# Loads of x on GpSimd's queue with eight half strips in place of five, in a convolutional attention and edge-filter kernel

## The chip, the cores and the metric

The kernel runs on one core of one Trainium2 chip. The metric is the time of one execution on the device in microseconds (us), as the median of several runs. The core has five engines that run at the same time, each with its own ordered stream of instructions: TensorE (PE, with its weight loads as PEld), VectorE (DVE), ScalarE (ACT), GpSimd (POOL) and SyncE (SP). SP computes nothing: it issues DMA transfers. POOL computes a little and issues transfers too. An engine carries out its stream strictly in order, so an instruction that waits holds up everything behind it on the same engine.

## What is computed

The input is x, four images of 512 channels by 64 x 64 pixels in float32. Two layers follow each other. Layer 0 is a linear attention over 8-channel heads, once on the projections q, k, v and once on their 5 x 5 depthwise convolution followed by a pointwise one, then a projection, a normalization and a residual. Layer 1 takes edge filters of layer 0's output, four branches, a channel attention, a fusing projection with a layer norm and again a residual.

```python
q, k, v = h @ wq.T, h @ wk.T, h @ wv.T                      # h: x with channels last
dw = conv(qkv, dw_kernel)                                   # 5x5, depthwise
pw = conv(dw, pw_kernel)                                    # 1x1, in groups of 8
f = concatenate([qkv, pw]).reshape(B, -1, 24, N)
query, key_, value = relu(f[:, :, :8]), relu(f[:, :, 8:16]), f[:, :, 16:]
scores = einsum('bhdn,bhen->bhde', value_pad, key_)         # value_pad: value and a row of ones
out = einsum('bhde,bhen->bhdn', scores, query)
out = out[:, :, :-1] / (out[:, :, -1:] + EPS)
y = batchnorm(conv(out, proj_kernel)) + x                   # layer 0
...
E = stack([sobel, lap, diag, grad])                         # edge filters of y
feat = gelu(batchnorm(einsum('kbchw,koc->kbohw', E, w_branch) + b_branch))
ef = feat * sigmoid(w_att2 @ gelu(w_att1 @ mean(feat)))
z = einsum('bchw,oc->bohw', ef, w_fuse) + b_fuse
return gelu(layernorm(z)) + y                               # layer 1
```

## The kernel before

**Groups and strips.** The 512 channels of q, k and v are cut into NG = 4 groups of 128, and an image's 4096 pixels into NJ = 8 strips of 512 (j = 0 to 7). The class `Group` (L231) does one group of one image: 16 groups in all, one after the other. A group first runs `keys_and_values`: for each strip in the order `KV_ORDER` (1, 0, 2, 3, ..., 7) a key projection (`project`, L274) and a value projection (`values`, L305). Then it runs `queries`: a query projection for each strip in the order `Q_ORDER` (6, 7, 5, 4, 3, 2, 1, 0). Pieces of other work stand between the projections: transposes, scores (L342), the convolution of the rolled image (`convolve`, L418), correlations (`correlate`, L473), `fold` (L371).

**x in SBUF.** A strip of x is 128 partitions by 4 x 512 floats. It is loaded as two half strips of 128 x 1024 floats, 512 KB each, by `load_x` (L260 to L266). All 16 half strips of image 0 stay in SBUF during its four groups (most of them in the pool `x_first`). For images 1 to 3 the half strips pass through the pool `xst` (L102), which has a fixed number of slots: a load waits until the last matmul that read the slot's former half strip is done. Strips 6 and 7 are kept from the values of a group to its queries, strips 1 and 0 from its queries to the keys of the next group; the others are loaded twice in a group. That makes 300 half strips for images 1 to 3, and 316 in all.

**Queues.** SP issues most loads and stores: x, weights, `near` (the values with their neighbours, L318 and L458), heads, and the data of the later stages. POOL issues four kinds: `flat<-strip` (L288, the projected strip to DRAM), `rolled<-flat` (L295, the strip back in the layout that the convolution wants), `y<-yt` (L686) and `ef<-ef_o` (L767). POOL also builds `mat` (L253) and adds in the last stage (L876, L897). In `project`, PE's projection goes to PSUM, ACT copies it (L281 for queries and L283) and POOL stores the copy (L288).

**Who sets the order.** PE's order is the order of the text (`manual_schedule` for PE alone). The streams of the other engines, SP and POOL among them, are put in order by the framework's scheduler when the program is built. It goes by the data that each instruction needs and by when it expects engines and slots to be free. It also gives each instruction its semaphore waits. The transfers of a queue take eight semaphores in turn, so a ninth waits for the first to have landed.

**Later stages beside the groups.** While the groups of image b run, `advance` gives out pieces of three later stages of image b - 1 by an expected pace: `project_out` (L677 on PE), `edge_branches` (L754 on PE, most of DVE's and ACT's work) and `fuse_out` (L866 and L882). The last image's stages run at the end, alone.

Of the kernel before, what the change touches and what calls it, by code (L numbers as in the profile page):

```python
# [89 lines left out]
def conv_seq_kernel(  # L90
    ctx: ExitStack, tc, x, wqkv, dpk, wtab, proj, projc, pwk, bn0, consts, vec, watt1, batt1, watt2, wbr, wfuse, out
):
    nc = tc.nc
# [5 lines left out]

    front = ctx.enter_context(ExitStack())  # L100
    keep = front.enter_context(tc.tile_pool(name="keep", bufs=1))
    xst = front.enter_context(tc.tile_pool(name="xst", bufs=5))  # L102
    mini = front.enter_context(tc.tile_pool(name="mini", bufs=2))
    gw = front.enter_context(tc.tile_pool(name="gw", bufs=2))
    vals = front.enter_context(tc.tile_pool(name="vals", bufs=VALS))
# [125 lines left out]
    class Group:  # L231
# [28 lines left out]
        def load_x(self, j):  # L260
            xs[self.b, j] = []
            for n in range(2):
                pool = x_first if self.b == 0 and j not in Q_ORDER[:2] else xst
                xt = pool.tile([P, 2, 512], F32, name="xt", tag="xt")
                nc.sync.dma_start(out=xt, in_=x[self.b, j, :, 2 * n : 2 * n + 2, :])
                xs[self.b, j] += [xt[:, 0, :], xt[:, 1, :]]  # L266

        def project(self, t, j):
# [873 lines left out]
```

## Time and profile before

| | us |
|---|---|
| median of 3 runs (4826.22 to 4835.85) | 4831.98 |
| the profiled execution | 4830.43 |
| its span, first to last instruction | 4828.6 |
| image 0's groups, 0 to 650: PE busy | 620.48 |
| beside image 0's later stages, 650 to 1705: PE busy of 1055 | 1007.72 |
| 1705 to 2890: PE busy of 1185 | 1121.17 |
| 2890 to 4110: PE busy of 1220 | 1138.13 |
| the last image's stages alone, 4110 to 4829: PE busy of 719 | 636.83 |

The granted TensorE clock is 0.968 over the span. The mean busy share of the DMA engines in these five stretches is 0.68, 0.77, 0.76, 0.75 and 0.54. Of the two queues in use, SP's moved 722.43 MB and POOL's 270.07 MB.

A line of a timeline gives start and length in us, the engine, the line of the program, the operation, the tile written and the tiles read, and how many instructions are merged in it. The bracket behind it is the idle time of the engine before it and what ended that idle time. A line of the waits gives who waited for whom, the total in us, how often, and the longest. A line of the DMA issues gives the tiles, the queue, the number of issues, the size of one and, for POOL's queue, the median time from issue to landing; for SP's queue the profile doesn't give that.

### The profile page before, as it was taken

The numbers are of one execution on the slowest core, as the hardware profiler recorded it, in microseconds if no ns is written. First come the engines' busy times: TensorE is split into PE (matmuls) and PEld (weight loads), VectorE is DVE, ScalarE is ACT, GpSimd is POOL, SyncE is SP. The second block draws the span as 40 slices with busy tenths as digits, with TensorE's granted clock in tenths as the row PEclk, the third lists the DMA queues.
The fourth block names the chain that finished last, engine by engine and source line by source line (L and its number), as shares of the span: only waits on it lengthen the run. The fifth ranks groups of instructions, "written<-read, shape, count | busy, mean of one in ns | idle before, by whom it ended". The sixth has DMA issues, their size and how long they took to land. (4 is left out here: it accounts for less than half of the span.)

```text
span 4828.6 us, 86405 instructions
## 1 busy us (share of the span) xinstructions
PE 4524.3 (94%) x35900; PEld 2461.5 (51%) x35900; DVE 2107.7 (44%) x2788; ACT 1588.7 (33%) x2719; POOL 987.7 (20%) x1291
## 2 busy tenths in 40 slices
PE   8999999998999999989899999988999999799987
PEld 5554554444566554444465655444446565344433
DVE  1222222114666634311356663441116666447966
ACT  2122121002554523300245452430014545214765
POOL 2111111111121224311111121431111211111443
PEclk9999999999999999999999999999999999899998
DMA  8666679667787877777678778758668887665445
GB/s 228 186 182 183 184 239 259 176 168 192 231 240 230 260 227 220 227 198 188 175 226 255 227 250 231 226 176 223 177 184 233 243 227 227 184 168 151 155 138 172
DMA packets 498327, 998.02 MB, mean 207 GB/s; under 512 B 189160, under 2 KB 221960, under 8 KB 479504
## 3 DMA queue, kind: packets, MB, share of 16 engines
q1 hardware_dynamic: 415760, 722.43, 50.6%
q0 software_dynamic: 82176, 270.07, 20.3%
q8 instruction: 283, 4.64, 0.4%
q14 instruction: 108, 0.88, 0.1%
HBM read 710.67 MB, written 281.61 MB: 206 GB/s over the span
## 5 line engine op out<-in xcount | busy, mean ns | idle before, releaser
L274 PE MATMUL proj<-xt,w_sb 128*128 128x512 f32 x2048 | 953.0, 608 | 50.3 <-DMA xt<-in_x 28.1
L677 PE MATMUL yps<-hd,fold_sb 128*128 128x512 f32 x2048 | 910.5, 600 | 35.8 <-DMA hd<-heads 27.8
L677 PEld LDWEIGHTS yps<-hd,fold_sb 128*128 128x128 f32 x2048 | 386.4, 192 | 531.7 <-issue 466.0
L274 PEld LDWEIGHTS proj<-xt,w_sb 128*128 128x128 f32 x2048 | 380.7, 194 | 541.7 <-issue 453.9
L418 PE MATMUL cv<-rolled,mat 64*32 64x504 f32 (+2 forms) x10240 | 576.4, 598 | 33.1 <-DMA rolled<-flat 19.1
L866 PE MATMUL zps<-ef,wf_sb 128*128 128x512 f32 (+1 forms) x1056 | 469.1, 597 | 45.6 <-DMA ef<-ef 16.7
L305 PEld LDWEIGHTS val<-w_sb,xt 128*128 128x128 f32 x4096 | 472.6, 193 | 43.4 <-issue 29.9
L305 PE MATMUL val<-w_sb,xt 128*128 128x128 f32 x4096 | 487.9, 278 | 2.4 <-DVE vt L312 1.9
L754 PE MATMUL br<-maps,wbr_sb 128*128 128x256 f32 (+1 forms) x1792 | 463.6, 412 | 0.0
L682 DVE SCALAR_TENSOR_TENSOR yt<-yps,shift,xr 128x512 f32<-128x512 f32 x128 | 95.7, 749 | 804.7 <-PE yps L677 757.8
L754 PEld LDWEIGHTS br<-maps,wbr_sb 128*128 128x128 f32 x1792 | 334.8, 189 | 137.4 <-issue 96.4
L288 POOL DMA_DIRECT2D flat<-strip x256 | 144.9, 566 | 1211.9 <-ACT strip L283 1184.8
L418 PEld LDWEIGHTS cv<-rolled,mat 64*32 64x32 f32 x10240 | 196.7, 109 | 381.9 <-issue 355.3
L295 POOL DMA_DIRECT2D rolled<-flat x512 | 273.3, 538 | 558.2 <-PE cv L418 519.5
L283 ACT COPY strip<-proj 128x512 f32<-128x512 f32 x256 | 149.0, 582 | 671.3 <-PE proj L274 671.3
L473 PE MATMUL corr<-near,ckt 128*32 128x160 f32 x8192 | 336.3, 318 | 26.4 <-DMA near<-near 26.2
L866 PEld LDWEIGHTS zps<-ef,wf_sb 128*128 128x128 f32 x1056 | 203.5, 196 | 293.8 <-issue 221.6
L473 PEld LDWEIGHTS corr<-near,ckt 128*32 128x32 f32 x8192 | 261.1, 112 | 122.0 <-issue 68.2
L686 POOL DMA_DIRECT2D y<-yt x128 | 114.4, 894 | 917.1 <-DVE yt L682 756.2
L730 DVE TENSOR_TENSOR maps<-dv 128x1054 f32<-128x1054 f32 (+1 forms) x112 | 159.8, 1427 | 256.8 <-PE br L754 256.7
L897 POOL TENSOR_TENSOR z<-z,yr 128x512 f32<-128x512 f32 (+1 forms) x132 | 175.5, 1348 | 272.7 <-ACT z L894 150.1
L333 ACT ACTIVATE kt<-tr 128x512 f32<-128x512 f32 x128 | 76.2, 595 | 466.4 <-PE tr L331 466.4
(131 smaller groups left out, 4466.0 us busy)
## 6 DMA issues: line engine op xcount, KB each, us to landing
xt<-in_x SPq DMA_DIRECT2D x316, 512.0 KB
near<-near SPq DMA_DIRECT2D x512, 264.0 KB
rolled<-flat POOLq DMA_DIRECT2D x512, 256.0 KB, 7.4
flat<-strip POOLq DMA_DIRECT2D x256, 256.0 KB, 5.8
win<-y SPq DMA_DIRECT2D x96, 396.0 KB
near<-vt SPq DMA_DIRECT2D x512, 66.0 KB
y<-yt POOLq DMA_DIRECT2D x128, 264.0 KB, 6.3
heads<-q SPq DMA_DIRECT2D x128, 256.0 KB
```

The lines of the kernel that those rows point to most:

```text
L274: nc.tensor.matmul(ps, lhsT=self.w[t][:, c, :], rhs=xs[self.b, j][c], start=(c == 0), stop=(c == NCH - 1))
L283: nc.scalar.copy(s, ps)
L288: nc.gpsimd.dma_start(out=self.flat[t][r, :, b : b + 8, :], in_=rows(s))
L295: nc.gpsimd.dma_start(out=self.rolled[t, half][r::8, :, :], in_=self.flat[t][r % 4, :, at : at + 8, :].rearrange("(n c) b w -> c n (b w)", ...
L305: nc.tensor.matmul(ps[:, ts(c, P)], lhsT=xs[self.b, j][n][:, ts(c, P)], rhs=self.w[VALUE][:, n, :], start=(n == 0), stop=(n == NCH - 1),)
L418: nc.tensor.matmul(rows(banks[2 * s + i])[32 * j : 32 * j + 32, :, c0:c1], lhsT=self.mat[t][q, 4 * s + j, (dx + 2) * 4 : (dx + 2) * 4 + 4, :],
L473: nc.tensor.matmul(self.banks[jj][32 * i : 32 * i + 32, 160 * b : 160 * b + 160], lhsT=self.held["c", i][:, at : at + 32], rhs=v[:, 4 * n ...
L677: nc.tensor.matmul(ps, lhsT=fold_sb[g // NG][:, g % NG, ts(c, P)], rhs=hd[g], start=(g == 0), stop=(g == 2 * NG - 1),)
L730: nc.vector.tensor_sub(flat[:, half : 3 * half - 2], dvs[:, 2 : 2 * half], dvs[:, 0 : 2 * half - 2])
L754: nc.tensor.matmul(rows(ps), lhsT=wbr_sb[:, k, c, :], rhs=rows(maps[:, slot[k], c % 2, :], WB)[:, :, 0:W], start=(c == 0), stop=(c == NCH ...
L866: nc.tensor.matmul(ps, lhsT=wf_sb[:, k, ts(c, P)], rhs=ef[k], start=(k == 0), stop=(k == 3))
L897: nc.gpsimd.tensor_add(rows(z), rows(z), rows(yr, WB)[:, :, 1 : W + 1])
```

## The change

The issue of an x load moves from SP to POOL for every image but the first, and the pool `xst` gets eight slots in place of five. Nothing else of the text changes.

```diff
@@ -99,7 +99,7 @@
     front = ctx.enter_context(ExitStack())
     keep = front.enter_context(tc.tile_pool(name="keep", bufs=1))
-    xst = front.enter_context(tc.tile_pool(name="xst", bufs=5))
+    xst = front.enter_context(tc.tile_pool(name="xst", bufs=8))
     mini = front.enter_context(tc.tile_pool(name="mini", bufs=2))
@@ -262,7 +262,7 @@
             for n in range(2):
                 pool = x_first if self.b == 0 and j not in Q_ORDER[:2] else xst
                 xt = pool.tile([P, 2, 512], F32, name="xt", tag="xt")
-                nc.sync.dma_start(out=xt, in_=x[self.b, j, :, 2 * n : 2 * n + 2, :])
+                (nc.gpsimd if self.b else nc.sync).dma_start(out=xt, in_=x[self.b, j, :, 2 * n : 2 * n + 2, :])
                 xs[self.b, j] += [xt[:, 0, :], xt[:, 1, :]]
```

PE's stream is the same before and after. In POOL's stream the 300 loads now stand among its stores and computations, where the scheduler put them. Around the end of the query strips of a group in the middle of image 1, POOL's stream then reads:

```
L288 DMACopy flat20_104<-strip_11116 128x512
L288 DMACopy flat20_104<-strip_11150 128x512
L265 DMACopy xt_11217<-in_x 128x1024
L265 DMACopy xt_11219<-in_x 128x1024
L265 DMACopy xt_11499<-in_x 128x1024
...
L265 DMACopy xt_11937<-in_x 128x1024
L288 DMACopy flat20_104<-strip_11228 128x512
```

Here `strip_11150` is the copy of the query projection of strip j = 2, and `xt_11217` and `xt_11219` are the two halves of strip j = 1.

## The prediction

> **What bounds the kernel now.** I read first the page's busy times, which say that TensorE (PE) is the bound:
>
> ```profile
> PE 4524.3 (94%) x35900; PEld 2461.5 (51%) x35900; DVE 2107.7 (44%) x2788; ACT 1588.7 (33%) x2719; POOL 987.7 (20%) x1291
> ```
>
> The span is 4828.6 us, so all that a better supply of data can return is 4828.6 - 4524.3 = 304 us. The chain that ended last covers only the final microseconds, so I went to the waits of PE, then to those of SP's queue (us in total, times, longest):
>
> ```profile
> PE proj L274 <- DMA xt<-in_x: 28.1, 4, 21.1
> PE yps L677 <- DMA hd<-heads: 27.8, 9, 10.5
> PE corr L473 <- DMA near<-near: 26.2, 11, 4.8
> ...
> SPq L265 <- PE proj L274: 270.9, 91, 16.3
> SPq L265 <- PE val L305: 225.3, 45, 25.6
> ```
>
> PE waits for x only 28.1 us in all, and 5.3 of it is the very first load, which the change leaves alone. In 650 to 4100 us, where images 1 to 3 run, it is 22.8 us in 3 waits, nearly all of it one. SP's queue does stand 270.9 + 225.3 = 496 us at L265 for a free slot, but that is time of a queue, not of PE.
>
> The big wait, in PE's timeline, and the load that ended it, in SP's (start, length):
>
> ```profile
> 3280.57 3.70 PE L274 MATMUL proj<-xt,w_sb 128*128 128x512 f32 x4 [21.12 <-DMA xt<-in_x]
> ...
> 3274.86 0.47 SPq L265 DMA_DIRECT2D xt<-in_x  x1
> ```
>
> This 512 KB load took 3280.57 - 3274.86 = 5.7 us from issue to use, on SP's queue.
>
> Then I set the changed program's order of instructions beside the timelines, at the place where a query strip of one group ends and the next begins (PE, ACT, POOL, SP around 1456 us):
>
> ```profile
> 1449.29 3.70 PE L274 MATMUL proj<-xt,w_sb 128*128 128x512 f32 x8
> 1452.92 2.54 PE L473 MATMUL corr<-near,ckt 128*32 128x160 f32 x64
> 1455.40 1.12 PE L371 MATMUL fold<-p,stt 128*128 128x512 f32 x2
> 1456.36 3.60 PE L274 MATMUL proj<-xt,w_sb 128*128 128x512 f32 x8
> ...
> 1455.76 1.17 ACT L750 ACTIVATE maps<-maps,sobel_eps 128x1048 f32<-128x1048 f32 x1
> 1456.83 0.58 ACT L281 ACTIVATE rq<-proj 128x512 f32<-128x512 f32 x1
> 1457.31 0.57 ACT L283 COPY strip<-proj 128x512 f32<-128x512 f32 x1
> ...
> 1458.18 0.55 POOL L288 DMA_DIRECT2D flat<-strip  x1 [9.46 <-ACT strip L283]
> ...
> 1437.73 0.33 SPq L265 DMA_DIRECT2D xt<-in_x  x1
> 1445.03 0.33 SPq L265 DMA_DIRECT2D xt<-in_x  x1
> ```
>
> The projection at 1449.29 is of strip j=2, the one at 1456.36 of j=1, seventh of the eight queries. Its two half strips were issued by SP at 1437.73 and 1445.03, well ahead. In the changed order both stand on POOL directly behind the store `flat<-strip` of j=2, which waits for ACT's copy, which waits for PE's projection of j=2. So they start no earlier than 1458.73, after PE wants them, though their slots were free at some 1428.
>
> **The change part by part.** *Eight slots for five* adds no instruction; it lets loads run up to four strips ahead. *The issues:* 300 half strips (316 less the 16 of image 0) leave SP, 300 x 0.35 us (median at L265) = 104 us, and with them the 496 us of slot waits; other loads of SP can only come earlier by that. PE's waits for SP's other loads in 650 to 4100 us are near 24.1, hd 17.3, ef 16.7 and watt 5.1 = 63 us; I count none as saved, as before the longest of them SP stood at L898 for POOL's z or at L318, not at L265. POOL gains 300 x 0.566 (the `flat` issue, also 128 rows) = 170 us: 988 to 1158, 24% of the span, on an engine that mostly waits. That costs nothing while POOL's next work has room; the built order also shows two more activation-table loads on ACT (1.28 us each), off the path too.
>
> *The wait removed:* the 21.1 us at 3280. In the new order that load stands far ahead (slot free at 3116, no late neighbour before it), so it goes. What is late next is `near`, whose last part was issued at 3260.4: used at 3284.2 before, it would be wanted at 3263.1 and land some 4 us after its issue, so about 3 us return. With the two small waits (1.7): gain 18 + 1 = 19 us.
>
> *The wait added.* For every xt of the new order I took the time of the POOL instruction ahead of it from the timeline, the time its slot came free (last matmul that read the slot's former tile), and the start of the matmul that wants it. Most have 20 us and more. Twelve strips don't, ten of them query j=1 of a group (all groups of images 1 to 3 but two). Start on POOL, then when PE wants it: 844.3/849.3 and 3129.8/3134.6 (second halves), 1242.2/1243.2, 1458.7/1456.4, 1672.3/1671.2, 1992.0/1994.9, 2413.5/2414.8, 2634.1/2635.2, 2851.8/2852.9, 2924.5/2929.2 (key j=3), 3822.2/3820.7, 4041.3/4041.3.
>
> The price hangs on the landing time of 512 KB on POOL's queue, which no row shows in these stages. The neighbours:
>
> ```profile
> rolled<-flat POOLq DMA_DIRECT2D x512, 256.0 KB, 7.4
> flat<-strip POOLq DMA_DIRECT2D x256, 256.0 KB, 5.8
> ...
> y<-yt POOLq DMA_DIRECT2D x128, 264.0 KB, 6.3
> ...
> ef<-ef_o POOLq DMA_DIRECT2D x16, 512.0 KB, 3.2
> ```
>
> Low end 3.2 us: the right size, but from the last stage, where DMA share is 0.54 against 0.75 to 0.77 here. High end 9.6: 7.4 plus 2.2 for another 512 KB at 222 GB/s. I take 7.0, since half the size took 5.8 to 7.4 on this queue in these stages and the full size 5.7 on SP's. Stall = start + 7.0 - wanted: 2.0, 2.2, 6.0, 9.3, 8.1, 4.1, 5.7, 5.9, 5.9, 2.3, 8.5, 7.0: sum 67 us. At 5.7 it is 51, at 9.6 it is 98, at 3.2 it is 26 (nine sites).
>
> The Trainium skill, "DMA: Bandwidth & Descriptors", section "Specifications", gives a first-byte latency of about 1 us for DMAs issued by GpSimd and 0.6 us by Sync, and its "Rules for kernel authors" say that spreading DMAs over queues saves only issue time, as all share 16 engines. The trace agrees on the issue time (POOL's is longer, 0.57 against 0.35 us) and can't show the latency by itself. By the page the load would land at 5.7 + 0.4 = 6.1 us, an estimate, and the sum would be about 56 us.
>
> *What the stalls hide.* Soon after five of these sites PE already waited for `near`, whose load is issued before the stall and gains by it: 4.8 (1256), 1.5 (1470), 3.1 (2864), 4.5 (3833), 2.2 (4056) = 16 us. These go. If the loads that now stand seven and eight in a row behind the late one slow `near`, this cover is gone, and 16 us come back.
>
> Sum: +67 - 16 - 19 = +32 us. The span is 4828.6, its execution 4830.4, the median 4832.0: 1.6 apart, so I set the sum on the median: 4864 us.
>
> **The rivals.** *A, the loads land in time (faster).* One mechanism: the late loads at the twelve sites land quickly, so that only the gain is left. It decides at a landing time of about 4 us, where stalls 34 - cover 14 - gain 19 = 0. For it: 3.2 us for 512 KB in the last stage. Against it: every median of POOL's queue in the crowded stages is above 5. With no stall: 4832 - 19 = 4813; if all 63 us of waits for SP's other loads fell too, 4750.
> *B, no difference.* Landing at 4 to 5 us, or some of SP's 63 us saved: 4832, within 10.
> *C, POOL's queue jams.* Bursts of eight loads (4 MB, 18.9 us at 222 GB/s) stand ahead of `flat` and `rolled`, and convolutions wait. For it: seven loads in a row behind each late one. Against it: from the last `rolled` issue to the convolution I read 12 to 20 us against 7.4 to land, and the bursts come when the next `rolled` is 20 us off. One convolution in each of 12 groups late by half a burst: 12 x 9.4 = 113, 4864 + 113 = 4977.
> *That the change does nothing* is excluded: the loads stand on POOL, eight deep.
>
> **How the numbers follow.** Forecast 0.72, A 0.13, B 0.10, C 0.05. The forecast's own range: landing 5.7 with the cover, 51 - 16 - 19 = +16 (4848), to landing 9.6 without it, 98 - 19 = +79 (4911). To hold 8 in 10 I reach down to 4828 (landing 3.2: 26 - 12 - 19 = -5, and B) and stop at 4900, leaving out A and the top. A measurement tells 0.2%, about 10 us, from no change: faster 0.13, same 0.10, slower 0.77.
>
> **What would show it.** PE proj waiting for xt: 22.8 us before in 650 to 4100, some 70 after, in about twelve waits of 2 to 9 us at the query before the last of each group, none of 21. PE corr's wait for near: 24 down to about 8. xt on POOL's queue: landing near 7 us. SP's waits at L265 gone. I am wrong if xt lands under 4 us, if the waits at j=1 are not there, or if PE's new time stands at convolutions (C) or SP's other loads.

## The result, and the profile after

The changed kernel takes 4963.24 us (median of 4 runs, 4953.84 to 4965.59) where the kernel before took 4832.64 beside it: 130.6 us more, a ratio of 1.0268 with a 95% interval of 1.0251 to 1.0286. The direction was forecast, the size was not: +32 had been the sum, and 4900 the top of the range. The profiled execution took 4960.89 us, its span is 4959.1 and the granted clock 0.960.

Busy times of the changed kernel:

```profile
PE 4545.5 (92%) x35900; PEld 2462.5 (50%) x35900; DVE 2104.5 (42%) x2788; ACT 1591.7 (32%) x2721; POOL 1143.5 (23%) x1591
```

PE is 21 us busier with the same matmuls, and 4959.1 - 4545.5 = 413.6 us idle in place of 304: some 109 us are new waits and 21 are slower matmuls. POOL is busy 156 us longer, near the forecast of 170; what that costs by itself no run shows. What PE waits for in the changed kernel:

```profile
PE proj L274 <- DMA xt<-in_x: 97.1, 19, 13.0
PE over L396 <- DVE rec L381: 36.4, 15, 11.6
PE corr L473 <- DMA near<-near: 25.5, 3, 11.5
PE cv L418 <- DMA rolled<-flat: 24.5, 5, 7.3
...
PE cv L418 <- DMA ef<-ef_o: 7.8, 1, 7.8
PE cv L418 <- DMA xt<-in_x: 6.7, 1, 6.7
```

The 21.1 us wait is gone, and x is now the largest wait all the same. `near` keeps its total, but as one wait of 11.5 us among three and not as many small ones. The reciprocals (17.2 before) are new in the list. The last two lines are waits for `rolled` as well: these two convolutions, at 757 and 2848 us, started directly after their last load of `rolled` had landed, 18.5 and some 23 us after its issue, where the median is 6.5 us. The profile puts the wait down to another transfer of POOL's queue that uses one of the same semaphores. So the convolutions waited 39.0 us for `rolled`, against 19.1 before. The landings on POOL's queue:

```profile
xt<-in_x POOLq DMA_DIRECT2D x300, 512.0 KB, 9.0
rolled<-flat POOLq DMA_DIRECT2D x512, 256.0 KB, 6.5
flat<-strip POOLq DMA_DIRECT2D x256, 256.0 KB, 4.5
```

One late strip, at the place that the prediction showed at 1456 us (timelines of PE, ACT and POOL of the changed kernel):

```profile
1480.95 3.70 PE L274 MATMUL proj<-xt,w_sb 128*128 128x512 f32 x8
...
1500.90 3.46 PE L274 MATMUL proj<-xt,w_sb 128*128 128x512 f32 x4 [12.72 <-DMA xt<-in_x]
1505.10 1.98 PE L274 MATMUL proj<-xt,w_sb 128*128 128x512 f32 x4 [0.73 <-DMA xt<-in_x]
...
1488.97 0.57 ACT L283 COPY strip<-proj 128x512 f32<-128x512 f32 x1
...
1489.84 0.55 POOL L288 DMA_DIRECT2D flat<-strip  x1 [9.46 <-ACT strip L283]
1490.38 3.67 POOL L265 DMA_DIRECT2D xt<-in_x  x7
```

The chain is the one that was forecast: POOL waits 9.46 us for ACT's copy, stores the strip, and only then issues seven loads in a row, the first of which PE wants at once. PE starts 1500.9 - 1490.4 = 10.5 us after that issue. Two things stand here that the prediction did not count. The second half strip is waited for again (0.73 us), and the first four matmuls take 3.46 us, where eight take 3.70 at 1480.95. The same stretch by windows, with the granted clock in the last column but two:

```profile
core 0: us, PE busy (x) PEld busy (x) DVE busy (x) ACT busy (x) POOL busy (x), PEclk, DMA share, GB/s
1470.00:1488.00 18.00, 16.50 (x118) 8.57 (x115) 15.04 (x19) 8.51 (x15) 5.05 (x9) 1.00 0.75 212
...
1500.80:1504.00 3.20, 3.10 (x4) 1.17 (x4) 0.00 (x0) 0.00 (x0) 0.00 (x0) 0.51 1.03 267
1504.00:1507.00 3.00, 2.27 (x5) 0.68 (x4) 0.00 (x0) 0.00 (x0) 0.00 (x0) 1.00 0.89 350
```

After the wait PE runs at a clock of 0.51 for some 3 us and then at 1.00 again: a long wait is paid a second time, at the restart.

**Where the time went.** PE's stream is the same in both kernels, so each matmul of one trace can be set against the same matmul of the other; the last one starts 131.5 us later. Sorted by the matmul in front of which the gap grew, with the places of the kernel before:

| part | forecast, us | measured, us |
|---|---|---|
| waits for late x strips (12 places forecast, 11 found) | +67 | +87.6 |
| extra time of the 8 matmuls after each of these waits | 0 | +28.3 |
| waits for `near` that these stalls hide | -16 | -16.0 |
| the wait at 3280, less what `near` takes back | -19 | -21.1 + 11.5 = -9.6 |
| everything else (rest of the sum) | 0 | +41.2 |

In "everything else" the largest are two waits for the reciprocal (+7.5 at 1367 and +11.6 at 3944), `watt_sb` (+8.3 at 2980), `rolled` and `ef` in front of a convolution (+6.9 at 2763), `maps` at 2547 (+5.8), and -10.5 for a load of heads at 2080. Of the 41.2 us, 9.4 had come about by 650 us, in image 0's groups, where only eight of the 300 moved loads are issued, four of them after 614 us. In e2 below, which has no load on POOL and loses nothing in all, it was 9.8. So this part can't be put down to loads on POOL.

### The profile page after: what moved, and what is told of

The parts are those of the page before. It is cut to its first block, busy times and chain, and to the rows that moved or that the text cites. A ratio compares the mean times of both kernels' runs of the same rounds, so it can differ in the third digit from the quotient of the medians.

```text
span 4959.1 us, 86522 instructions
## 1 busy us (share of the span) xinstructions
PE 4545.5 (92%) x35900; PEld 2462.5 (50%) x35900; DVE 2104.5 (42%) x2788; ACT 1591.7 (32%) x2721; POOL 1143.5 (23%) x1591
## 3 DMA queue, kind: packets, MB, share of 16 engines
q1 hardware_dynamic: 372560, 565.12, 38.7%
## 5 line engine op out<-in xcount | busy, mean ns | idle before, releaser
L274 PE MATMUL proj<-xt,w_sb 128*128 128x512 f32 x2048 | 970.4, 617 | 119.3 <-DMA xt<-in_x 97.1
L274 PEld LDWEIGHTS proj<-xt,w_sb 128*128 128x128 f32 x2048 | 384.9, 196 | 623.7 <-issue 529.4
L473 PE MATMUL corr<-near,ckt 128*32 128x160 f32 x8192 | 331.7, 315 | 29.0 <-DMA near<-near 25.5
L281 ACT ACTIVATE rq<-proj 128x512 f32<-128x512 f32 x128 | 76.1, 595 | 510.8 <-PE proj L274 448.5
```

The lines of the kernel that those rows point to most:

```text
L274: nc.tensor.matmul(ps, lhsT=self.w[t][:, c, :], rhs=xs[self.b, j][c], start=(c == 0), stop=(c == NCH - 1))
L473: nc.tensor.matmul(self.banks[jj][32 * i : 32 * i + 32, 160 * b : 160 * b + 160], lhsT=self.held["c", i][:, at : at + 32], rhs=v[:, 4 * n ...
```

## The experiments

Every run is compared with runs of the kernel before on the same chip; the ratio is what counts, since the kernel before itself took 4803 to 4832 us there. Four columns sum up the profiles: PE's wait for x at its projections (L274 in the kernel before), for `near` and for the reciprocal, and SP's wait for the store `near<-vt` at the loads of `near` (L458). Lines of runs with added text have higher numbers.

| run | x loads of images 1 to 3 | ratio (95%) | x | near | rec | SP near<-vt |
|---|---|---|---|---|---|---|
| before | SP, 5 slots | 1 | 28.1 | 26.2 | 17.2 | 68.8 |
| after | POOL, 8 slots | 1.0268 (1.0251 to 1.0286) | 97.1 | 25.5 | 36.4 | 132.4 |
| e1 | POOL, 5 slots | 1.0444 (1.0416 to 1.0473) | 195.4 | 34.1 | 14.3 | 100.4 |
| e2 | SP, 8 slots | 0.9990 (0.9974 to 1.0005) | 5.3 | 29.3 | 17.2 | 67.7 |
| e3 | POOL, j=1 on SP | 1.0156 (1.0121 to 1.0191) | 44.1 | 26.5 | 45.0 | 139.9 |
| e4 | POOL, asked for one strip earlier | 1.0127 (1.0097 to 1.0156) | 24.4 | 53.1 | 35.3 | 138.1 |
| e5 | POOL, two strips earlier | 1.0087 (1.0057 to 1.0118) | 12.8 | 49.1 | 35.6 | 129.8 |
| e6 | ACT | 1.0125 (1.0088 to 1.0162) | 5.4 | 32.8 | 23.5 | 93.2 |
| e7 | keys POOL, queries SP | 1.0066 (1.0043 to 1.0089) | 10.2 | 20.8 | 40.3 | 124.0 |
| e8 | POOL, the store flat on ACT | 1.0166 (1.0127 to 1.0206) | 31.1 | 57.4 | 22.7 | 116.7 |
| e9 | as e5, a quarter of the bytes | 0.9916 (0.9891 to 0.9941) | 5.5 | 21.7 | 17.2 | 69.4 |
| e10 | as e2, a quarter of the bytes | 0.9885 (0.9856 to 0.9914) | 5.0 | 15.1 | 17.2 | 45.3 |
| e11 | as e5, win on ACT | 1.0089 (1.0066 to 1.0112) | 14.8 | 41.2 | 25.8 | 143.7 |
| e12 | queries POOL, keys SP | 1.0044 (1.0021 to 1.0067) | 8.3 | 38.7 | 19.1 | 79.5 |
| e13 | as after, a quarter of the bytes | 1.0040 (1.0020 to 1.0060) | 56.9 | 14.8 | 17.2 | 58.8 |

A wait that the table leaves out is that of the convolutions for transfers of POOL's queue: 19.1 us before, 39.0 after, 25.1 in e2, 43.0 in e5, 28.3 in e6, 42.1 in e7, 21.7 in e12, 24.4 in e9 and 21.0 in e10.

### The two parts of the change, each alone (e1, e2)

```diff
 # e1, against the changed kernel
-    xst = front.enter_context(tc.tile_pool(name="xst", bufs=8))
+    xst = front.enter_context(tc.tile_pool(name="xst", bufs=5))
 # e2, against the changed kernel
-                (nc.gpsimd if self.b else nc.sync).dma_start(out=xt, ...
+                nc.sync.dma_start(out=xt, ...
```

> The issue engine alone is changed (loads of images 1 to 3 on POOL), the five slots stay. Theory (the loss is loads of x that stand on POOL behind a store or a copy that waits for the strip just computed, and so start too late; every stall costs start + landing - wanted): with five slots far fewer loads can be placed early. Set against the times of the kernel before, the built order has some 54 half strips with less than 9 us from their start to their use, 353 us in all at a landing of 9 us (197 at 5.7), counting both halves of a strip, so perhaps two thirds of it in PE's waits. Expected 5000 to 5180 us, and PE proj waiting for xt 180 to 350 us. Rival 1 (POOL's queue is at fault by its load alone, 300 loads of 512 KB in a FIFO with flat and rolled, wherever they stand): as the changed kernel, 4940 to 4980. Rival 2 (the eight slots are at fault, bursts of prefetches that take DMA from near and rolled): as the kernel before, 4820 to 4850.

> The eight slots alone, loads on SP as before. Theory (loss is in the issue order on POOL): no half strip of the built order has under 12 us from start to use, so the 21 us wait for xt at 3280 goes, near behind it gives some 11 back, and nothing is added: 4810 to 4830, faster than before by 0 to 0.5%. Rival 1 (POOL's queue by its load): the same, 4810 to 4830. Rival 2 (slots, bursts of prefetches): most of the 130 us stay, 4900 to 4965.

e1 took 5047.73 us and waits 195.4 us for x in 22 waits, both within its forecast. That the issue on POOL costs 4.4% with five slots and 2.7% with eight excludes rival 2: the slots do not hurt, they give the loads room. e2 confirms it from the other side. With eight slots on SP the 21.1 us wait is gone and nothing of the 130 us is there; the gain of 0.1% is no more than the measurement can tell from none.

### Earlier loads on the same queue (e3, e4, e5, e8)

```diff
 # e3: the late strips alone on SP
+                (nc.gpsimd if self.b and j != 1 else nc.sync).dma_start(out=xt, ...
 # e4: in project(), ahead of the matmuls
+            if t == QUERY and self.b and j != Q_ORDER[-1]:
+                ahead = Q_ORDER[Q_ORDER.index(j) + 1]
+                if (self.b, ahead) not in xs:
+                    self.load_x(ahead)
 # e5: as e4, with
+                ahead = Q_ORDER[min(Q_ORDER.index(j) + 2, len(Q_ORDER) - 1)]
 # e8: the store of the strip leaves POOL
-            nc.gpsimd.dma_start(out=self.flat[t][r, :, b : b + 8, :], in_=rows(s))
+            nc.scalar.dma_start(out=self.flat[t][r, :, b : b + 8, :], in_=rows(s))
```

> As the changed kernel, but the strips j=1 (the seventh query of a group, where ten of the twelve late strips were) are loaded from SP; 263 of 300 loads stay on POOL. Theory: by the built order the late sites of j=1 are gone; what is left with under 9 us is some 11 half strips near 1700-1730, 2433 and 2890-2915, 54 us at a landing of 9 us, of which some 35 reach PE. With the early loss in image 0 of 10 us and near's 11 against the 21 gained: 4850 to 4890. Rival 1 (POOL's queue by its load, 263/300 of the loss): 4940 to 4965. Rival 2 (slots): 4940 to 4970.

> As the changed kernel, with all 300 loads on POOL in eight slots, but the kernel's text asks for the next query strip's load one projection earlier, so that it stands ahead of the store of the strip just computed and not behind it. Theory: the leads at j=1 rise from some -2 to 3 us to some 4 to 11; at a landing of 9 us 44 us are short over both halves (14 at 7 us), of which some 30 reach PE: 4850 to 4890, and PE proj waiting for xt some 30 us in place of 97. Rival 1 (POOL's queue by its load): no change, 4940 to 4980. Rival 2 (slots): no change, 4940 to 4980.

> As the changed kernel (300 loads on POOL, eight slots), but the text asks for the strip after the next query strip, so that by the built order only 5 half strips have under 9 us from start to use (13 us in all), in place of 23 (164 us). Theory 1 (late strips are the whole loss): PE proj waits for xt under 15 us and the time is 4820 to 4845. Theory 2 (late strips are about half of it; the other half is that loads free of SP's order go out in bursts and take the DMA engines from SP's store near<-vt, so the reads near<-near that wait for it come late, pile up and hold up win and the reciprocals behind it): xt under 15 us as well, but SP's L458 waiting for near<-vt stays at 130 to 140 us (68.8 before), PE's waits for near stay at 45 to 60 and for rec at some 35, and the time stays at 4870 to 4895.

> As the changed kernel, but the store flat<-strip goes out on ACT's queue, directly behind the copy that makes the strip; the loads of x stay on POOL. It takes away the instruction that eight of the eleven late strips stood behind; three (behind ef<-ef_o at 2635 and 2853, y<-yt at 849) stay. Theory: half strips with under 9 us fall from 23 (164 us) to 15 (61 us); PE proj waiting for xt 97 down to 30 to 50, the time 4885 to 4920. Rival (the landing of 9 us and up in POOL's queue, and not what stands ahead of the load, makes them late): xt stays at 80 to 100 and the time at 4940 to 4970.

All 300 loads stay on POOL in e4, e5 and e8, and the time falls by 1.4, 1.8 and 1.0% of the kernel before. So the queue's load by itself (rival 1) is not the cause of that part: what counts is behind which instruction the load stands. e8 is the most direct: only the store is taken from in front of the loads, and the wait for x goes from 97.1 to 31.1 us, as forecast. e4, at 4893.22 us, lies just above its 4850 to 4890. e3 was slower than forecast (4905.02 against 4850 to 4890); 270 of its loads were on POOL, not 263. Two places that the built order showed as late stayed (in the times of the kernel before): 13.2 us at 2913, a key strip behind `ef<-ef_o`, and 6.8 us at 1731.

e5 separates two causes. The waits for x are at 12.8 us, 5.3 of them the first load of all, and still 0.87% remains: 4859.89 us, some 10 under theory 2's 4870 to 4895 and above theory 1's 4820 to 4845. The kernel before took 4810.35 us there; 1.0087 of 4832 would be 4874, inside theory 2's range. The waits are those that theory 2 named, and one that it did not name, of convolutions behind POOL's queue:

```profile
PE corr L477 <- DMA near<-near: 49.1, 10, 15.0
PE over L400 <- DVE rec L385: 35.6, 15, 10.9
...
PE cv L422 <- DMA xt<-in_x: 17.1, 2, 9.5
...
PE proj L278 <- DMA xt<-in_x: 12.8, 5, 5.3
```

The line of the convolutions stands for `rolled` again: its last loads in front of the two waits landed 19.5 and 24.4 us after their issue. With the other waits for `rolled` (25.9) that is 43.0 us, 17.9 more than in e2, where `near` and the reciprocal have 19.8 and 18.4 less than here (waits for heads and `ef` on SP fell by 5 and 12). So of the 2.68%, 2.68 - 0.87 = 1.81% are late strips with what follows them, some 87 us of 4832, and the rest is another loss.

### What the other loss is made of (e6, e7, e12, e11)

SP's wait in front of the loads of `near`, in the kernel before and in the changed one:

```profile
SPq L458 <- DMA near<-vt: 68.8, 35, 5.6
```

```profile
SPq L458 <- DMA near<-vt: 132.4, 35, 10.5
```

SP writes the values to DRAM (`near<-vt`) and reads them back with their neighbours (`near<-near`). The read waits for the store to land; that wait doubles when the loads of x leave SP. Part of that may be only SP arriving earlier, now that no loads stand in between. What it leads to is seen at one of the two waits for the reciprocal (SP and DVE of the changed kernel):

```profile
1366.91 5.62 SPq L458 DMA_DIRECT2D near<-near  x8
1372.63 0.45 SPq L708 DMA_DIRECT2D win<-y  x1
...
1379.45 3.18 SPq L318 DMA_DIRECT2D near<-vt  x4
1382.72 6.97 SPq L708 DMA_DIRECT2D win<-y  x1
...
1391.17 0.71 DVE L723 TENSOR_TENSOR dv<-win 128x528 f32<-128x528 f32 x1 [8.56 <-DMA win<-y]
...
1392.41 3.35 DVE L381 RECIPROCAL rec<-rec 128x512 f32<-128x512 f32 x1
```

Eight reads of `near` go out in a pack, and the load of `win` directly behind them takes 0.45 us. The next one, behind four stores `near<-vt`, takes 6.97 us to issue where the median is 0.38; DVE waits 8.56 us for it, and the reciprocal for which PE waits stands behind on DVE. At the other wait for the reciprocal, at 4065 us, it is the same: four stores in 8.42 us, then a load of `win` that takes 4.75, for which DVE waits 12.66. In e2 the issue of the same load as at 1382 takes 0.54 us, behind four stores too. So the pack of reads, which theory 2 had in mind, is not what holds `win` up; what does was not tried.

```diff
 # e6: the loads on ACT's queue
-                (nc.gpsimd if self.b else nc.sync).dma_start(out=xt, ...
+                (nc.scalar if self.b else nc.sync).dma_start(out=xt, ...
 # e7 (keys) and e12 (queries), on top of e5
+        def load_x(self, j, eng=None):
...
+                (eng or nc.sync).dma_start(out=xt, ...
...
+                self.load_x(j, nc.gpsimd if self.b else nc.sync)    # e7
...
+                    self.load_x(ahead, nc.gpsimd)                   # e12
 # e11, on top of e5: win off SP
-                nc.sync.dma_start(
+                nc.scalar.dma_start(
                     out=win,
```

> As the changed kernel, but the 300 loads are issued on ACT's queue in place of POOL's; in the built order they stand alone or in pairs between ACT's work and none has under 12 us from start to use. Theory 2 (loads off SP's order compete with near's store, whatever the engine): few or no waits for xt, SP's L458 waiting for near<-vt well above 68.8 if they still go out in bursts, about as before if they are spread; 4850 to 4895 with bursts, 4815 to 4840 without. Rival (POOL's queue itself, its landing in order with flat and rolled): 4815 to 4840, rolled and flat landing as before (7.4 and 5.8), and near's store unchanged. Against both: a load that waits for its slot holds up ACT's copies and Relu behind it, which PE then waits for (ACT strip L283, rq L281): 4900 and more.

> Half of the move: the key strips' loads (156) are issued on POOL, the query strips' (144) on SP, asked for two strips ahead as in the run before. By the built order 2 half strips have under 9 us (7 us in all). Theory 2 (contention of loads that are free of SP's order): the key loads form the long bursts (up to 8), the query loads on SP stand in order with near, so part of the loss stays: 4840 to 4870, SP's L458 waiting for near<-vt between 70 and 130 us. Theory 1 (late strips only): 4820 to 4840.

> The other half of the move: the query strips' loads (144) on POOL, asked for two strips ahead, in runs of at most 4; the key strips' loads stay on SP. Theory 2 (the long bursts are the key strips' loads, when all eight slots come free): most of the 1.0066 that the key half cost does not show, 1.000 to 1.004, SP's L458 waiting for near<-vt 65 to 85 us. Rival (any load that leaves SP costs the same): half of 1.0087 and up, 1.004 to 1.007, 100 us and up.

> As the run with 300 loads on POOL asked for two strips ahead, but the 112 loads of win are issued on ACT's queue and not on SP's, so that they stand behind no packed reads near<-near. Theory 2 (win is held up on SP, DVE waits for it, the reciprocal stands behind it on DVE and PE behind that): PE's wait for rec falls from 35.6 to some 17 (17.2 before), both 8 to 11 us waits gone, 4835 to 4850 us. Rival (the reciprocals come late for another reason, a new order on DVE): rec stays at 35, 4855 to 4870.

e6 has no waits for x beyond the first, nearly all its loads stand alone or in pairs, and POOL issues none of them; it is 1.25% slower. So a loss of this size arises without POOL and without long bursts, and the rival of e6 falls; but theory 2 had forecast 4815 to 4840 us without bursts, and that was missed too (4875.67). ACT's copies of the strips stood 16.4 us behind loads; how much of the loss that makes was not told apart, so that it is the same loss as e5's is not shown. e7 is within its forecast. e12, at 1.0044, lies at the line between the two forecasts of the time; SP's wait for `near<-vt`, 79.5 us, is in theory 2's 65 to 85. The query half costs something too: with e7's 1.0066 the halves add up to more than e5's 1.0087, though within the intervals. The convolutions' wait for `rolled` goes with the keys' loads: 42.1 us with the keys on POOL, 21.7 with the queries there.

e11 is a miss that teaches something. The two long waits for the reciprocal shrink from 7.5 and 10.9 us to 5.0 and 3.7, and the sum to 25.8 where 17 had been forecast; the time is the same as e5's: 1.0089 against 1.0087, and above the forecast's 4835 to 4850. At these two places PE gained 2.4 and 7.2 us against e5; others grew, a load of heads at 4359 by 8.5, one at 2093 by 6.0, a convolution behind POOL's queue at 751 by 4.2. The place of a wait can be moved without the loss moving.

### How much of it is bytes (e9, e10, e13)

```diff
                 xt = pool.tile([P, 2, 512], F32, name="xt", tag="xt")
+                if self.b:
+                    nc.gpsimd.dma_start(out=xt[:, :, 0:128], in_=x[self.b, j, :, 2 * n : 2 * n + 2, 0:128])
+                    xs[self.b, j] += [xt[:, i, 0:128].unsqueeze(1).to_broadcast([P, 4, 128]) for i in range(2)]
+                    continue
```

e10 has `nc.sync` there. All three leave out three quarters of each load and use the rest four times. With the smaller transfers the scheduler also moves some instructions of POOL, DVE and SP; the streams of PE stay the same.

> As the run with 300 loads on POOL asked for two strips ahead (4859.9 us), but each load of images 1 to 3 carries a quarter of its columns (128 KB in place of 512), and the matmuls read that quarter four times: the output is not the reference's. The number of loads and their queue stay; the bytes of x fall to a quarter. Theory 2a (what is left of the loss is bytes: bursts of loads crowd the 16 DMA engines while near, rolled and ef are wanted): the loss against the same kernel with the loads on SP (next run) falls from 0.97% (1.0087 against 0.999) to under 0.3%, and SP's L458 waiting for near<-vt falls to some 70 to 90 us. Theory 2b (it is order: near's reads, win and the reciprocals come in another order once the loads leave SP, or loads stand ahead of rolled and flat on POOL): the loss stays at 0.6 to 1%, with the waits for rec at 30 to 36 us and near's long one at 15.

> The same quarter loads on SP's queue, with eight slots (output not the reference's): the counterpart of the run before. Both theories: faster than the kernel before by 0 to 1%, 4790 to 4835 us, since less is transferred. What counts is the difference of the two runs: under 15 us for theory 2a, 30 to 45 us for theory 2b.

> The changed kernel itself, with each load of images 1 to 3 at a quarter of its bytes (output not the reference's); the built order has the same 23 half strips with under 9 us from start to use as the changed kernel. Against the run of the same quarter loads asked for early (0.9916 of before) it shows what the late strips cost when a load is short. Theory (the price of a late strip is the landing of its bytes among others plus a slow restart of PE; with quarter loads the landing was 5.4 us in the median, not 9.0): waits of PE proj for xt near 48 us (leads of the twelve sites against 5.4), 0.999 to 1.003 of before, so the late strips cost some 0.75 to 1.1% where they cost 1.8% with full loads (1.0268 against 1.0087). Rival (the price is the late start alone, the store and POOL's waits ahead of the load, whatever the bytes): waits for xt stay at 85 to 97 us, and the time at 1.008 to 1.011 of before.

With full loads POOL (e5) stands 0.97% behind SP (e2); with quarter loads e9 stands 0.31% behind e10, 14.2 us, and the spans of the two profiled executions are equal (4770.8 and 4770.9). The waits for the reciprocal are back at 17.2, SP's wait for `near<-vt` is at 69.4 (45.3 in e10), and the convolutions' wait is 24.4. So most of the second loss goes with the bytes of x, as theory 2a said. With the order moved as well, and intervals of 0.25 to 0.3% on each ratio, that rests on two runs and not on a clean cut; and fewer bytes also shorten what stands ahead of `rolled` in POOL's own queue, which these runs don't tell apart from competition between the queues.

e13 keeps the late order and shortens the loads. PE's wait for x:

```profile
PE proj L278 <- DMA xt<-in_x: 56.9, 10, 10.5
```

The landing is 4.9 us in the median, and 48 us had been worked out from the prediction's own starts. The late strips cost 1.0040 - 0.9916 = 1.24% here and 1.81% with full loads: between the two forecasts of the time, which both missed (the interval of 1.0040 reaches into the first). The restart is here too (PE and POOL):

```profile
1454.85 5.23 PE L278 MATMUL proj<-xt,w_sb 128*128 128x512 f32 x8 [8.42 <-DMA xt<-in_x]
...
1448.09 0.55 POOL L292 DMA_DIRECT2D flat<-strip  x1 [9.46 <-ACT strip L287]
1448.63 5.65 POOL L266 DMA_DIRECT2D xt<-in_x  x8
```

Eight matmuls take 5.23 us here, not 3.60 to 3.70; nine such places carry 17.4 us more than before in the eight matmuls after the wait. By the waits for x (56.9, against 48 and 85 to 97) it is the landing that was too small in my sum, and not the late start alone.

## Why the prediction was wrong in size

The sum was +32 and the traces have +131.5. Of the 99.5 us between them, 20.6 are the waits for late strips, sized too small; 28.3 the restart, put at nothing; 9.4 what `near` took back at one place; and 41.2 the rest, put at nothing as well.

**What bounds the kernel; slots; POOL's time.** Right, as far as the runs show. Eight slots alone cost nothing (e2). POOL's 156 us were not tried by themselves; in e5, which has the same 300 issues, the whole loss is 0.87%.

**The wait removed (-18, with small ones -19).** The wait went, but the step "so about 3 us return" for `near` failed: 11.5 us returned, so -9.6. The step took a landing of 4 us and the issue time of before for `near`'s last part; by its own figures that is 3260.4 + 4 - 3263.1 = 1.3 us, not 3. The issue time was the larger error: set against the moment when PE wanted it, `near`'s last part was issued 2.7 us ahead in this sum and 5.2 us behind in the changed kernel (3369.8 against 3364.6), and PE started 6.2 us after the issue. SP issued it behind a store of `z`, for which it had waited 6.8 us for POOL (4.2 before). In e2, where the loads stay on SP, `near` takes 2.5 us more at this place; in e5 the wait there is 15.0. What it meets there was not tried by itself.

**The wait added (+67).** Right in mechanism: of the twelve places ten stalled, those at 2929 and 3133 did not, and one at 1750 that had not been listed did. The term was mis-sized. I took 7.0 us from issue to landing for all of them; at the eleven places PE began its work 6.0 to 12.4 us after the issue on POOL, 10.5 in the median, above my upper bound of 9.6. (That bound was added up wrongly: 512 KB at 222 GB/s are 2.4 us and not 2.2, and from 256 to 512 KB only 256 KB are added.) The place of a load in a run of loads (each issued within 1.5 us of the one before) does not explain it. The medians by place in the changed kernel are 7.1, 8.6, 11.1, 10.9, 15.1, 16.3 and 17.5 us from the first to the seventh (225 loads with a recorded landing), but all eleven late loads were the first of their run: 7.0 was a fair figure for first places, and not for these. What goes with it is SP's traffic at that moment. Between issue and landing, SP's queue took 0.36 to 0.46 of the transfer engines' time at the seven places with over 10 us, and 0.14 to 0.34 at the four with 6.0 to 7.5 us. That is a comparison of eleven places; no run changed SP's traffic there. e13 puts a number on the size alone: with a quarter of the bytes at the same places the wait for x is 56.9 and not 97.1.

**The missing term.** The restart, +28.3 us over eleven places, 2.6 each, second halves' waits included. It stood in the prediction's own fences: after the 21 us wait at 3280.57 four matmuls took 3.70 us, and at 1449.29 eight took 3.70; the granted clock at 3280 to 3284 was 0.50. I quoted both lines and priced every new wait at its idle time alone. The Trainium skill, "TensorE: Matmul & The Clock Gate", section "Part 1: The HAM clock gate", has it as a rule: after an idle window of about 3.4 us TensorE runs at half rate until about 3.4 us of work have passed. The rows agree (0.51 for some 3 us after a wait of 12.72). By the rule a restart costs 1.7 us, and eleven cost 19, an estimate; the trace has more, though there was none after the shortest wait (2.81 us, clock 1.00 behind it).

**What the stalls hide (-16).** Right: all five waits are gone, -16.0.

**SP's other loads (0).** Wrong in sign. I asked whether they could come earlier and counted nothing; they came later. In "everything else" (+41.2) the waits for them grew by some 30 us from 650 us on: the reciprocals behind `win` 19.1, `watt_sb` 8.3, `near` at other places 6.0, heads -3.1. The convolutions' waits for POOL's own `rolled` grew by another 15, 9.4 us stem from image 0, and the balance, some -13, is smaller differences, most of them waits that fell. That the loads of x, which no longer wait their turn on SP, compete with these transfers is what e9 and e10 speak for; e5's 0.87% is the price of all this when x itself is no longer late. Which transfers lose how much was not settled: e11 shows that shortening some of the waits does not give their time back.

**The rivals.** A fell: at no late place was x there within 4 us. C gave the nearest number (4977), mostly for another reason. Its mechanism is there, but smaller: the convolutions' wait for `rolled` went from 19.1 to 39.0 us, some 15 of it in images 1 to 3, where C had 113. Against C I had set 12 to 20 us of room against a median landing of 7.4 us; at two places the last load of `rolled` took 18.5 and some 23. My answer to the rule that the prediction quotes from the Trainium skill, "DMA: Bandwidth & Descriptors", section "Rules for kernel authors", that queues share 16 engines, was to use it for issue time; e9 and e10 speak for the sharing itself as most of what it cost beyond the late strips.

Summed with the measured sizes: 87.6 + 28.3 - 16.0 - 9.6 + 41.2 = 131.5.

## What to carry to other kernels

A load that moves to another queue is late by what stands in front of it there: read the built order, and if it stands behind a store that waits for the result just computed, ask for it two steps earlier (here 1.8 of 2.7%). Price a new wait of a matmul engine at its idle time plus a restart at half clock (here 2.6 us each in the mean), and the landing, as far as these eleven places show, by what else is being transferred at that very moment, not by a median over the kernel. And a queue in which loads wait their turn also paces them: freed of it, the loads here made transfers late that had been on time.

## What the hardware showed that was not expected

The clock fell to half after a wait of 5.0 us, and stayed there for longer than 3 us. At 1267 in the changed kernel PE waited 5.02 us, then the four matmuls of each half strip took 3.75 and 3.73 us, with a second wait of 0.91 us between them; the clock was 0.50 from 1267 to 1275. So the shorter wait lost as much at the restart (4.8 us, the 0.91 among them) as in the wait. The line between waits that cost a restart and waits that don't was not sharp: in e13 the clock was 0.50 after a wait of 2.95 us (at 2414), shorter than the 3.4 us of the rule, and 1.00 after one of 3.00 (at 2641). A single DMA issue on SP took up to 6.97 us where the median of its line is 0.38; in e2, at another place, one took 4.23, and in the kernel before an x load took 5.82. Why an issue takes so long was not tried.
